# A hand-ordered four-layer kernel: last front stores issued by GpSimd, front loads asked for a period ahead, four page turns first, one norm sum on VectorE, new keys' shares on ScalarE

## The chip, the cores and the metric

One Trainium2 chip, one of its cores. The metric is device microseconds (us) of one execution, median of the runs shown. Everything is float32.

## The reference, cut to what matters

Four residual layers follow each other on x, 64 sequences of 32 tokens with 512 features:

```python
x = x + einsum('bct,bcd->bdt', x, W0[cond])            # a 32x32 mix of the tokens of each sequence
x = x + x @ base_w.T + base_b + (x @ A[adapt].T) @ Bw[adapt].T      # LoRA, rank 16
# attention with a paged cache: 32 query heads, 8 key heads, D = 128
q, k, v = x @ Wq.T, x @ Wk.T, x @ Wv.T
q = rope(rmsnorm(q, q_norm_w), pos); k = rope(rmsnorm(k, k_norm_w), pos)
k_all = concat(k_cache[block_table], k); v_all = concat(v_cache[block_table], v)   # 512 + 32 keys
p = softmax(where(valid, q @ k_all.T / sqrt(D), -1e30))
x = x + (p @ v_all) @ Wo.T
x = x + einsum('bct,bcd->bdt', x, W3[cond])
```

rmsnorm(t, w) is t * rsqrt(mean(t*t) + eps) * w; rope multiplies by a cosine, a half-swapped copy by a sine, and adds the two.

## The kernel before

**Tiles.** The 2048 tokens are 16 tiles (`t`) of 128 tokens, four sequences each. The key heads are taken in two groups `g` of four. A *unit* is one sequence with one group of key heads (128 units), and it takes four *slots*, one for each key head: 512 slots, 0 to 511, in which TensorE does scores, transposes of the probabilities and the product with the values. In the same slots the projections of the next pair of tiles are done (a pair has 32 slots): seven blocks of products with sums of weights (`block_sum`), their results taken from one PSUM bank (`proj_ps`) by `Block.take` on VectorE, then normed and rotated by class `Norm`.

**The front.** Slots -43 (`begin`) to -1 hold everything ahead of the first scores: layers 1 and 2 of all 16 tiles (class `First`), the turning of group 0's cached keys, 16 pieces of 128 rows (class `Turn`: load `page_rows`, four transposes into the one PSUM tile `s_ps`, copy back by ScalarE, store to DRAM as `kT`), the rotary tables (`rotary`, stored as `rot`), and the projections of the first pair. A tile of `First` starts every two slots; its slot `home` is -39 + 2t. Its steps are load, mix and add; `turn_x` (four transposes of x into the PSUM tile tagged "tx") and `keep_x` (ScalarE's copy to `x1T`); `ranks` (x1T times the LoRA factors, four products, also tagged "tx"); `linear` (chunks 0 to 4 into `l_ps`); the second `add`; `turn_out` and `keep_out` (PSUM tag "to"); `store_x`, `store`, and for odd tiles `sums` and `store_sums`. An even tile also turns its LoRA rows, `turn_a`/`keep_a`, through the same tag "to". Every PSUM tile named here has one buffer.

**What sets the order.** Nothing is scheduled by the compiler: each engine runs its instructions in the order in which they were emitted. `at(slot, where, do)` puts a call on a list, and `slot(i)` emits slot i in a fixed order of lists: fetch (SyncE's loads), pool (GpSimd), scores and flips of the attention, "pe", "power", one `norm_piece`, "turn", values, the division of the softmax, "dve", two more `norm_piece`, "keep", "act", "store". A call that waits holds up all that was emitted after it on the same engine; SyncE (SP) issues most transfers, GpSimd (POOL) the gathers and some weights. `norm_piece` takes the next of the queued VectorE pieces of the norms, at most two in a slot together with the takes counted in `busy`.

**Memory.** `x_sb` has 4 buffers, `page_rows` 4, `rot` 2, `rot_b` 2, `x_12` and `x_34` (the sums) 1. The pools of the front are closed at slots -7 (`start`) and -2 (`first`), and the attention's tiles `pen`, `sm`, `v_sb`, `v_new` lie in their memory: the first writer of these waits until the last reader of the old tiles is done. `Unit` issues 16 loads of `kT`, `Unit.mask` writes `pen` on GpSimd, which the first VectorE operation on the scores (`tensor_tensor_reduce`, L825) reads.

Of the kernel before, what the change touches and what calls it, by code (L numbers as in the profile page):

```python
# [43 lines left out]
P = 128  # L44
# [4 lines left out]
D = 128  # L49
# [28 lines left out]
def resid_kernel(  # L78
# [149 lines left out]
    with ExitStack() as l2:  # L228
# [161 lines left out]
        class First:  # L390
# [121 lines left out]

            def store_x(self):
                nc.sync.dma_start(out=x_dram[self.t], in_=self.x)

            def store(self):
                nc.sync.dma_start(out=xT_dram[self.t], in_=self.x2T)

            def store_sums(self):
                for i in (0, 1):  # L520
                    nc.sync.dma_start(out=xS_dram[self.t // 2][:, i], in_=self.s[i])
# [154 lines left out]
        class Norm:  # L676
# [35 lines left out]
            def swapped(self):  # L712
                which = 3 if self.k is None else 1
                self.b = proj_pool.tile([P, REP, D], F32, name="rot_b", bufs=2)
                half = D // 2
                for i in (0, 1):
                    nc.vector.tensor_tensor(
                        self.b[:, :, i * half : (i + 1) * half],
                        self.raw[:, :, (1 - i) * half : (2 - i) * half],
                        self.step.rot[:, which, i * half : (i + 1) * half]  # L720
                        .unsqueeze(1)
                        .to_broadcast([P, REP, half]),
                        ALU.mult,
                    )

            def sum(self):
                nc.gpsimd.tensor_tensor(self.a, self.a, self.b, ALU.add)  # L727
# [24 lines left out]
        class Unit:  # L752
# [85 lines left out]
            def divide(self, k):  # L838
# [4 lines left out]
                nc.vector.tensor_scalar(self.new[:, k, :], sm[:, L:], share, None, ALU.mult)  # L843
# [85 lines left out]
        def norm_piece(slot):  # L929


            if not pieces or pieces[0][0] > slot or busy.get(slot, 0) >= 2:
                return
# [3 lines left out]
            if norm:  # L937
                norm.sum()
                slot += 2
# [6 lines left out]
        def begin_norm(slot, norm):  # L946
# [3 lines left out]
            for piece in (norm.scale, norm.straight, norm.swapped):  # L950
                pieces.append((slot + 2, piece, norm if piece == norm.swapped else None))
# [30 lines left out]
        for i in range(n_pairs):  # L982
# [19 lines left out]
            if p == 0:  # L1002
# [3 lines left out]
                for w, what in zip((-1, 0, 2, 5) if g == 0 else (-12, -11, -10, -9), (3, 2, 1, 4)):  # L1006
                    at(home + w, "dve", block_sum, KV, what)
            if p == NT // 2 - 1:
# [14 lines left out]
        for t in range(NT):  # L1023
# [3 lines left out]
            at(home - 3 if t > 1 else begin, "fetch", call, *f, "load")  # L1027
            at(max(begin, home - 4), "pool", call, *f, "fetch")
# [11 lines left out]
            at(home + 2, "pe", call, *f, "linear", (0, 1, 2))  # L1040
            at(home + 3, "pe", call, *f, "linear", (3, 4))
            at(home + 3, "power", call, *f, "add")
            at(home + 4, "store", call, *f, "store_x")
            at(home + 4, "turn", call, *f, "turn_out")
            at(home + 4, "keep", call, *f, "keep_out")
            at(home + 5, "store", call, *f, "store")
            if t % 2:
                at(home + 5, "dve", call, *f, "sums")
                at(home + 6, "store", call, *f, "store_sums")
# [7 lines left out]
        for c in range(NT):  # L1057

            home = -27 + c
            key = -1 - c  # L1060
            at(home - 2 if c > 3 else begin + 8, "fetch", make, turn_of, key, Turn, 0, c, start_pool, 4)
            at(home, "turn", call, turn_of, key, "turn")
# [4 lines left out]
        for u in range(len(units)):  # L1067
            at(KG * (u - 1) if u > 1 else ready + 2 * u, "fetch", make, unit_of, u, Unit, u)
# [114 lines left out]
        with tc.manual_schedule(engines=ENGINES):  # L1183
# [20 lines left out]
            for j in (0, 1):  # L1204
                at(begin + 3, "store", load_kv_weights, 0, 1, j)
                at(begin + 4, "store", load_kv_weights, 0, 0, j)
# [243 lines left out]
```

## Time and profile before

| what | value |
|---|---|
| runs | 2533.17 us median of 3 (2532.82 to 2536.7) |
| profiled execution, its own time | 2537.45 us |
| its span, first to last instruction | 2535.6 us |
| TensorE busy | 2464.5 us (97%) |
| VectorE, ScalarE, GpSimd busy | 1717.2, 1305.9, 1303.7 us |
| slot 0's first scores start at | 204.83 us |
| last slots end, output projection begins | about 2150 us |

The span is told from the first instruction, and the execution's own time is 1.85 us longer. The profiled execution was 4.3 us slower than the median of the runs. "PE" is TensorE's products and transposes, "PEld" its weight loads, "SPq" SyncE's issue of transfers; "a <- b" says that a waited, and that b was what came last.

### The profile page before, as it was taken

To read this page: it belongs to the slowest core of one execution; us is meant where nothing else is said; L and a number is where in the kernel's file an instruction comes from. 1 tells how busy PE (TensorE), PEld (TensorE's weight loads), DVE (VectorE), ACT (ScalarE), POOL (GpSimd) and SP (SyncE) were. 2 spreads that over 40 slices of the span, in tenths; PEclk is the share of its full clock that TensorE was granted. 3 is DMA by queue.
4 is the path that set the end of the run, shared out by engine and by line. 5 is a ranking of instruction groups with operands and counts; after the bars stand their busy time and mean duration, and the time that the engine had idled before them with its cause. 6 is when DMAs were issued, how large, how long until landed. Compare 5 with 4: busy or idle time off the path is not lost.

```text
span 2535.6 us, 46991 instructions
## 1 busy us (share of the span) xinstructions
PE 2464.5 (97%) x13760; PEld 1861.5 (73%) x13760; DVE 1717.2 (68%) x4114; ACT 1305.9 (52%) x3623; POOL 1303.7 (51%) x1086
## 2 busy tenths in 40 slices
PE   7997999999999999999999999999999999999999
PEld 4554777777777776677777777777777778888887
DVE  6645877777777786888777777778777766433222
ACT  1234666666666665666666666666666654000000
POOL 4434666666656565666565666666566763000000
PEclk9998999999999999999999999999999999999999
DMA  6875666666666667766566656565657685333221
GB/s 228 271 224 159 184 199 191 196 185 197 185 191 188 195 190 225 216 200 184 176 188 183 186 168 190 170 186 170 189 170 219 214 277 155 126 108 127 100 84 59
DMA packets 442846, 459.68 MB, mean 181 GB/s; under 512 B 50720, under 2 KB 367008, under 8 KB 434784
## 3 DMA queue, kind: packets, MB, share of 16 engines
q1 hardware_dynamic: 393488, 294.38, 38.1%
q0 software_dynamic: 49104, 162.31, 21.1%
q8 instruction: 112, 1.84, 0.3%
q14 instruction: 142, 1.16, 0.2%
HBM read 385.18 MB, written 79.69 MB: 183 GB/s over the span
## 4 chain that ended last, share of the span: by engine, by line
PE 88%; DVE 5%; DMA 4%; SPq 1%; issue 1%; ACT 0%; POOL 0%; ACTq 0%; DVEq 0%; POOLq 0%
PE proj_ps L630 21%; PE o_ps L872 17%; PE out_ps L1274 14%; PE s_ps L817 10%; PE s_ps L820 8%; PE pT_ps L859 8%; PE head_ps L735 3%; PE o_ps L884 2%; PE l_ps L478 2%; DVE p_new L843 1%; DMA kT<-page_rows 1%; DVE sm L825 1%; DMA v_sb<-v,v_rows 1%; DMA x_sb<-in_x 1%; PE s_ps L852 1%
## 5 line engine op out<-in xcount | busy, mean ns | idle before, releaser
L872 PEld LDWEIGHTS o_ps<-pT,v_sb 128*128 128x128 f32 x4096 | 520.4, 192 | 135.2 <-issue 124.1
L105 POOL DMA_INDIRECT v_sb<-v,v_rows x512 | 525.6, 1027 | 182.1 <-PE o_ps L872 77.1
L825 DVE CUSTOM_DVE_ANT_0 sm<-s_ps,pen 128x544 f32<-128x544 f32 x512 | 369.4, 721 | 365.6 <-PE s_ps L820 250.4
L836 ACT ACTIVATE sm<-sm,top 128x544 f32<-128x544 f32 x512 | 382.2, 746 | 414.0 <-DVE top L825 305.9
L872 PE MATMUL o_ps<-pT,v_sb 128*128 128x128 f32 x4096 | 541.8, 275 | 5.9 <-DMA v_sb<-v,v_rows 5.5
L842 ACT ACTIVATE sm<-sm,share 128x512 f32<-128x512 f32 x512 | 369.9, 722 | 172.3 <-DVE share L841 139.5
L693 POOL TENSOR_TENSOR rstd<-ss,minus_half 128x4 f32<-128x4 f32 x160 | 198.5, 1241 | 368.0 <-DVE ss L691 365.5
L817 PE MATMUL s_ps<-kT,qT 128*128 128x288 f32 x1024 | 350.6, 424 | 13.7 <-DVE top L825 13.4
L861 DVE COPY pT<-pT_ps 128x512 f32<-128x512 f32 x512 | 350.6, 685 | 3.9 <-PE o_ps L872 1.5
L820 PE MATMUL s_ps<-kT,qT 128*128 128x256 f32 x1024 | 306.3, 381 | 2.5 <-DMA kT<-kT 2.5
L859 PE MATMUL pT_ps<-ident,sm 128*128 128x128 f32 x2048 | 308.2, 273 | 0.5 <-DVE pT L861 0.5
L727 POOL TENSOR_TENSOR rot_a<-rot_a,rot_b 128x512 f32<-128x512 f32 x160 | 205.6, 1285 | 197.2 <-DVE share L841 148.5
L859 PEld LDWEIGHTS pT_ps<-ident,sm 128*128 128x128 f32 x2048 | 256.4, 141 | 53.2 <-DVE pT L861 1.7
L788 POOL TENSOR_SCALAR pen<-key_f,seq_f 128x544 f32<-128x544 f32 x128 | 276.3, 2158 | 22.0 <-DMA xS<-x 11.0
L686 ACT ACTIVATE sq<-raw 128x128 f32<-128x128 f32 x640 | 198.1, 309 | 82.2 <-DVE raw L642 52.3
L820 PEld LDWEIGHTS s_ps<-kT,qT 128*128 128x128 f32 x1024 | 195.6, 191 | 57.3 <-issue 3.0
L642 DVE TENSOR_TENSOR raw<-proj_ps,raw 128x512 f32<-128x512 f32 x336 | 225.4, 682 | 8.4 <-PE proj_ps L630 6.0
L843 DVE TENSOR_SCALAR p_new<-sm,share 128x32 f32<-128x32 f32 x512 | 209.7, 410 | 18.1
L630 PE MATMUL proj_ps<-sum,x 128*128 128x512 f32 x384 | 192.1, 603 | 1.9 <-DVE raw L642 1.9
L105 POOL DMA_INDIRECT mix_rows<-in_w,cond_rows x32 | 33.7, 1055 | 309.0 <-DVE mix_diag L171 301.4
L817 PEld LDWEIGHTS s_ps<-kT,qT 128*128 128x128 f32 x1024 | 155.6, 192 | 33.2 <-DVE top L825 15.9
L1324 ACT COPY p<-out_ps 128x256 f32<-128x256 f32 x7 | 2.6, 372 | 333.1 <-PE out_ps L1274 333.1
(158 smaller groups left out, 3417.9 us busy)
## 6 DMA issues: line engine op xcount, KB each, us to landing
kT<-kT SPq DMA_DIRECT2D x2048, 64.0 KB
o<-oT SPq DMA_DIRECT2D x29, 1024.0 KB
o_in<-o SPq DMA_DIRECT2D x28, 1024.0 KB
rot<-rot SPq DMA_DIRECT2D x48, 256.0 KB
page_rows<-in_kv_cache SPq DMA_DIRECT2D x32, 256.0 KB
vn<-raw SPq DMA_DIRECT2D x32, 256.0 KB
v<-in_kv_cache SPq DMA_DIRECT2D x32, 256.0 KB
kT<-page_rows SPq DMA_DIRECT2D x32, 256.0 KB
```

The costliest lines, as they stand in the source:

```text
L105: nc.gpsimd.indirect_dma_start(out=dst, out_offset=None, in_=table, in_offset=bass.IndirectOffsetOnAxis(ap=index, axis=0),)
L630: nc.tensor.matmul(self.ps, lhsT=self.pair.x[x][:, c if x == "b" else half.start + c, :], rhs=blocks(self.b)[w][:, c, :], start=(c == 0), ...
L788: nc.gpsimd.tensor_scalar(self.pen, key_f, seq_f[:, self.b : self.b + 1], BIG, ALU.is_ge, ALU.mult)
L817: nc.tensor.matmul(ps[:, first:HID], lhsT=q, rhs=self.kT[:, :n1, k, :], start=True, stop=True)
L820: nc.tensor.matmul(ps[:, HID : first + LA], lhsT=q, rhs=self.kT[:, n1:, k, :], start=True, stop=True)
L825: nc.vector.tensor_tensor_reduce(out=sm, in0=ps[:, first : first + LA], in1=self.pen, scale=1.0, scalar=3e38, op0=ALU.add, op1=ALU.min, ac ...
L836: nc.scalar.activation(sm, sm, AF.Exp, bias=top, scale=-1.0, accum_out=total)
L842: nc.scalar.activation(sm[:, :L], sm[:, :L], AF.Copy, scale=share)
L859: nc.tensor.transpose(ps[:, c, :], self.sm[k][:, c * P : (c + 1) * P], ident)
L861: nc.vector.tensor_copy(pT, ps)
L872: nc.tensor.matmul(self.o_ps[k], lhsT=self.v[c][:, k * D : (k + 1) * D], rhs=self.pT[k][:, c, :], start=(c == 0), stop=False,)
L1274: nc.tensor.matmul(ps[:, :HALF], lhsT=o[:, i, :], rhs=w[i // REP][:, i % REP, :], start=(i == 0), stop=(i == KG * REP - 1),)
```

## The change

Eight edits. (1) The stores of the last three tiles of the front go through GpSimd's queue. (2) x of a tile is loaded at `home - 4` instead of `home - 3`, a page at its slot - 3 instead of - 2, with 5 buffers; `linear` and all that follows it is one slot earlier; tile 1's gathers are at `begin`. (3) Pages 0 to 3 are loaded at `begin` and turned in slots -40 to -37, at the head of the "pe" list from the second on, instead of in slots -27 to -24. (4) The key and value weights are loaded two slots later, and unit 1's `kT` one slot later. (5) The last sum of a norm is a fourth VectorE piece instead of a GpSimd operation, the heads are turned one slot after it instead of two, and `rot_b` has one buffer. (6) The new keys' shares are made by ScalarE. (7) Slots with a `block_sum` count as full for the norm pieces, every fourth slot may have one more piece, and (8) the key and value sums of group 1 stand in slots 204, 207, 210 and 213 instead of 211 to 214.

```diff
--- before.py
+++ after.py
@@ -510,15 +510,19 @@
                 if p == 0:
                     pair_of[0].x["12"], pair_of[0].x["34"] = s, r
 
+            def queue(self):
+
+                return nc.sync if self.t < NT - 3 else nc.gpsimd
+
             def store_x(self):
-                nc.sync.dma_start(out=x_dram[self.t], in_=self.x)
+                self.queue().dma_start(out=x_dram[self.t], in_=self.x)
 
             def store(self):
-                nc.sync.dma_start(out=xT_dram[self.t], in_=self.x2T)
+                self.queue().dma_start(out=xT_dram[self.t], in_=self.x2T)
 
             def store_sums(self):
                 for i in (0, 1):
-                    nc.sync.dma_start(out=xS_dram[self.t // 2][:, i], in_=self.s[i])
+                    self.queue().dma_start(out=xS_dram[self.t // 2][:, i], in_=self.s[i])
 
         lora = {}
         last_scores = []
@@ -711,7 +715,7 @@
 
             def swapped(self):
                 which = 3 if self.k is None else 1
-                self.b = proj_pool.tile([P, REP, D], F32, name="rot_b", bufs=2)
+                self.b = proj_pool.tile([P, REP, D], F32, name="rot_b")
                 half = D // 2
                 for i in (0, 1):
                     nc.vector.tensor_tensor(
@@ -724,7 +728,7 @@
                     )
 
             def sum(self):
-                nc.gpsimd.tensor_tensor(self.a, self.a, self.b, ALU.add)
+                nc.vector.tensor_tensor(self.a, self.a, self.b, ALU.add)
 
             def turn(self):
                 if "o" in room:
@@ -840,7 +844,7 @@
                 share = small.tile([P, 1], F32, name="share")
                 nc.vector.reciprocal(share, self.total[k])
                 nc.scalar.activation(sm[:, :L], sm[:, :L], AF.Copy, scale=share)
-                nc.vector.tensor_scalar(self.new[:, k, :], sm[:, L:], share, None, ALU.mult)
+                nc.scalar.activation(self.new[:, k, :], sm[:, L:], AF.Copy, scale=share)
 
             def flip_new(self):
 
@@ -929,14 +933,13 @@
         def norm_piece(slot):
 
 
-            if not pieces or pieces[0][0] > slot or busy.get(slot, 0) >= 2:
+            if not pieces or pieces[0][0] > slot or busy.get(slot, 0) >= 2 + (slot % 4 == 1):
                 return
             busy[slot] = busy.get(slot, 0) + 1
             _, piece, norm = pieces.pop(0)
             piece()
             if norm:
-                norm.sum()
-                slot += 2
+                slot += 1
                 while slot in turning or (slot - VLAG) % KG == KG - 1:
                     slot += 1
                 turning.add(slot)
@@ -947,8 +950,8 @@
 
             at(slot, "act", norm.squares)
             at(slot + 1, "power", norm.power)
-            for piece in (norm.scale, norm.straight, norm.swapped):
-                pieces.append((slot + 2, piece, norm if piece == norm.swapped else None))
+            for piece in (norm.scale, norm.straight, norm.swapped, norm.sum):
+                pieces.append((slot + 2, piece, norm if piece == norm.sum else None))
 
         def begin_block(pair, b, slots):
             block = Block(pair, b)
@@ -1003,8 +1006,10 @@
                 sums = [(b, what) for b in (0, 1) for what in (3, 2, 1)] + [(0, 4), (1, 4)]
                 for w, one in zip((5, 6, 7, 9, 10, 11, 17, 18), sums):
                     at(home + w, "dve", block_sum, *one)
-                for w, what in zip((-1, 0, 2, 5) if g == 0 else (-12, -11, -10, -9), (3, 2, 1, 4)):
+                    busy[home + w] = busy.get(home + w, 0) + 2
+                for w, what in zip((-1, 0, 2, 5) if g == 0 else (-19, -16, -13, -10), (3, 2, 1, 4)):
                     at(home + w, "dve", block_sum, KV, what)
+                    busy[home + w] = busy.get(home + w, 0) + 2
             if p == NT // 2 - 1:
 
                 if g == NG - 1:
@@ -1024,8 +1029,8 @@
             home = -WINDOW - AHEAD - 6 + 2 * t
             f = [first_of, t]
             at(home - 5 if t > 1 else begin, "fetch", make, *f, First, t)
-            at(home - 3 if t > 1 else begin, "fetch", call, *f, "load")
-            at(max(begin, home - 4), "pool", call, *f, "fetch")
+            at(home - 4 if t > 1 else begin, "fetch", call, *f, "load")
+            at(max(begin, home - 4) if t > 1 else begin, "pool", call, *f, "fetch")
             at(home - 2, "dve", call, *f, "diagonal")
             at(home - 1, "pe", call, *f, "mix")
             at(home - 1, "power", call, *f, "add")
@@ -1037,16 +1042,16 @@
             at(home + 1, "pool", call, *f, "bias")
             at(home + 1, "pe", call, *f, "ranks")
             at(home + 1, "power", call, *f, "own_ranks")
-            at(home + 2, "pe", call, *f, "linear", (0, 1, 2))
-            at(home + 3, "pe", call, *f, "linear", (3, 4))
-            at(home + 3, "power", call, *f, "add")
-            at(home + 4, "store", call, *f, "store_x")
-            at(home + 4, "turn", call, *f, "turn_out")
-            at(home + 4, "keep", call, *f, "keep_out")
-            at(home + 5, "store", call, *f, "store")
+            at(home + 1, "pe", call, *f, "linear", (0, 1, 2))
+            at(home + 2, "pe", call, *f, "linear", (3, 4))
+            at(home + 2, "power", call, *f, "add")
+            at(home + 3, "store", call, *f, "store_x")
+            at(home + 3, "turn", call, *f, "turn_out")
+            at(home + 3, "keep", call, *f, "keep_out")
+            at(home + 4, "store", call, *f, "store")
             if t % 2:
-                at(home + 5, "dve", call, *f, "sums")
-                at(home + 6, "store", call, *f, "store_sums")
+                at(home + 4, "dve", call, *f, "sums")
+                at(home + 5, "store", call, *f, "store_sums")
 
             home = SLOTS * t + 9
             turning.add(home)
@@ -1056,16 +1061,20 @@
             at(home + 1, "store", call, turn_of, t, "store")
         for c in range(NT):
 
-            home = -27 + c
+
+            home = -27 + c if c > 3 else begin + 3 + c
             key = -1 - c
-            at(home - 2 if c > 3 else begin + 8, "fetch", make, turn_of, key, Turn, 0, c, start_pool, 4)
-            at(home, "turn", call, turn_of, key, "turn")
+            at(home - 3 if c > 3 else begin, "fetch", make, turn_of, key, Turn, 0, c, start_pool, 5)
+            where = "turn" if c > 3 else "pe"
+            at(home, where, call, turn_of, key, "turn")
+            if 0 < c < 4:
+                plan[home, where].insert(0, plan[home, where].pop())
             at(home, "keep", call, turn_of, key, "keep")
             at(home + 1, "store", call, turn_of, key, "store")
             at(begin + 11 + c, "dve", rotary, c)
             at(begin + 11 + c, "store", store_rotary, c)
         for u in range(len(units)):
-            at(KG * (u - 1) if u > 1 else ready + 2 * u, "fetch", make, unit_of, u, Unit, u)
+            at(KG * (u - 1) if u > 1 else ready + 3 * u, "fetch", make, unit_of, u, Unit, u)
             at(KG * (u - 1) + 1 if u else -1, "pool", call, unit_of, u, "mask")
             for c in range(NC):
                 at(KG * u - 1 + c, "pool", call, unit_of, u, "fetch_values")
@@ -1202,8 +1211,8 @@
             nc.gpsimd.dma_start(out=lora["base"], in_=base_w)
             nc.gpsimd.dma_start(out=lora["bias"], in_=across(base_b, HID))
             for j in (0, 1):
-                at(begin + 3, "store", load_kv_weights, 0, 1, j)
-                at(begin + 4, "store", load_kv_weights, 0, 0, j)
+                at(begin + 5, "store", load_kv_weights, 0, 1, j)
+                at(begin + 6, "store", load_kv_weights, 0, 0, j)
             for c in range(2 * KG):
                 at(begin + 9 + c, "store", load_q_weights, 0, c // 2, c % 2)
             for i in range(begin + 1, begin + 11):
```

## Prediction

> **What bounds the kernel now.** First the page's busy shares and the row of slices, then the stages, then TensorE's waits in them.
>
> ```profile
> PE 2464.5 (97%) x13760; PEld 1861.5 (73%) x13760; DVE 1717.2 (68%) x4114; ACT 1305.9 (52%) x3623; POOL 1303.7 (51%) x1086
> PE   7997999999999999999999999999999999999999
> PEclk9998999999999999999999999999999999999999
> ...
> 104.00:170.00 66.00, 59.09 (x238) 33.58 (x237) 32.78 (x82) 20.61 (x60) 25.08 (x21) 0.95 0.78 245
> 180.00:200.00 20.00, 16.91 (x61) 8.49 (x59) 10.18 (x23) 6.74 (x23) 4.92 (x5) 0.98 0.36 113
> 200.00:220.00 20.00, 6.99 (x15) 3.35 (x14) 4.74 (x8) 3.67 (x11) 5.80 (x5) 0.67 0.48 149
> 300.00:400.00 100.00, 100.00 (x603) 75.18 (x602) 74.94 (x190) 64.45 (x175) 60.44 (x50) 1.00 0.65 189
> 1020.00:1040.00 20.00, 16.06 (x91) 11.20 (x89) 19.03 (x36) 10.34 (x30) 12.82 (x10) 1.00 0.78 246
> ```
>
> Columns of a stage: its length, busy time of PE, PEld, DVE, ACT, POOL, then the clock, the DMA share and GB/s. From 240 to 2150 us TensorE is the bound: in 300:400 it never idles, while VectorE has a quarter and ScalarE a third of the time free. So work moved between those engines is worth nothing there; time can come from the front (0 to 240) and from the few stages where TensorE idles, such as 1020:1040 (4 us, VectorE at 95%). In the front three things stand out.
>
> The largest hole is at the handover to the attention. In order of time (start, duration, engine, line, what it had waited for):
>
> ```profile
> 190.53 9.37 SPq L773 DMA_DIRECT2D kT<-kT  x16
> 201.80 9.34 SPq L773 DMA_DIRECT2D kT<-kT  x16
> 212.96 0.85 SPq L521 DMA_DIRECT2D xS<-x  x2
> 217.48 2.12 POOL L788 TENSOR_SCALAR pen<-key_f,seq_f 128x544 f32<-128x544 f32 x1 [10.99 <-DMA xS<-x]
> 220.41 1.33 PE L817 MATMUL s_ps<-kT,qT 128*128 128x288 f32 x2 [12.64 <-DVE top L825]
> ```
>
> SyncE issues 32 loads of kT, 0.59 us each, ahead of the last sums' store (212.96). `pen` lies in their memory, so GpSimd waits for that store to land, VectorE for `pen`, and TensorE 12.64 us for the one `s_ps`.
>
> The second is SyncE's queue between 104 and 170 us. Its waits (total, times, longest) and TensorE's there:
>
> ```profile
> SPq L256 <- DMA kT<-page_rows: 29.9, 11, 5.0
> SPq L399 <- DMA x<-x_sb: 25.0, 11, 5.6
> PE s_ps L272 <- DMA page_rows<-in_kv_cache: 3.6, 3, 2.4
> PE mix_ps L424 <- DMA x_sb<-in_x: 3.3, 3, 2.0
> ```
>
> A page's load stands behind the landing of the kT store that frees its buffer. From one page load to the one two later takes SyncE 13.6 us (107.87, 121.46, 135.01), TensorE wants 10.4 (turns of x2T at 73.09, 82.60, 93.97, 104.34). Over the five tiles from 104.34 to 169.35 the loss is 65.0 - 5 x 10.4 = 13 us. The third is the start: TensorE is busy 6.2 of the first 20 us.
>
> [...] clock 0.67 in 200:220, and four projection products take 3.78 us at 201.25 against 1.88. [...] p_new (L843) has median 242 and maximum 1358 ns, mean 410.
>
> **The change part by part.** Negative is faster.
>
> *Ring: stores through GpSimd, one slot earlier, unit 1 one slot later.* Ten DMAs leave SyncE; on GpSimd, at about 0.6 us of issue each (its base and bias issues), they are 6 us, in a stage in which it is busy 5 of 20. Behind them in its order stand `bias`, `power`, the gathers and `pen`, and each store waits for VectorE's `add` or `sums` or ScalarE's copy, all made a slot before it. The last sums go out in slot -4 instead of at 212.96, land some 4 us later (212.96 to 217), before `pen` comes up in slot -1. Removed: the wait of 12.6, and the half clock behind it (220.41 to 226: 0.7 + 0.5 + 0.9 + 0.7 + 0.3 = 3). What is late next is VectorE's chain of take, squares and norm, which already makes TensorE wait 2.31 + 0.79 at 197 to 201; I leave that. x2T of tile 15 moves one slot earlier, but the slots after it are thin and bound by that chain: 1.5 us more. Sum -17; bounds -8 (pen then waits for something else by half) and -20.
>
> *Pages and x a slot ahead, four pages first.* The kT waits fall from 11 to 7, since pages 5 to 8 take buffers freed early; SyncE still falls behind in those 7 slots by (13.6 - 10.4)/2 = 1.6, 11 us in all, but a load now has 3 slots (15.6 us) for a store and a load of 4.4 + 3.2 us: 8 us of slack instead of 3. Of the 13 lost some 10 come back; bounds -4 and -13. The turns of four pages, 0.44 us each on TensorE, move to slots -40 to -37, where TensorE waits anyway (3.4 us for a_rows before 13.15): -2.
>
> *Start.* The gather of tile 1's mix rows, issued at 9.34 behind the 1 MB of base weights and landed at 18.5, goes ahead of them, and 2 MB of weights go later. Against that, page 1's turn waits for ScalarE's copy of page 0 out of the one `s_ps`, page 2's for page 1's, with `ranks` and `linear` behind them in TensorE's order; and SyncE waits for each copy before it stores the page, with the weights, x of tile 3 and later stores behind. The weights then go out at about 20 us, the first sum of them is taken at 38.8. I take -2; bounds -6 and +4.
>
> *Two new waits of TensorE.* Before, chunks 3 and 4 of `linear` (1.72 us) stand between `turn_x` and `ranks` and cover ScalarE's copy. After, they come ahead of `turn_x`, and `ranks` follows it directly. And `turn_out` of an even tile now stands in the same slot as the next even tile's `turn_a`, both through "to", so `turn_a` waits for `keep_out`. The trace has the parts:
>
> ```profile
> 34.07 0.60 PE L441 MATMUL x1T_ps<-ident,x_sb 128*128 128x128 f32 x4
> 35.02 0.59 ACT L457 COPY x1T<-x1T_ps 128x512 f32<-128x512 f32 x1
> 35.37 1.02 PE L478 MATMUL l_ps<-b_rows,hT 128*128 128x512 f32 x2
> ```
>
> The next product could start 0.44 us after the turn starts (34.51); the copy lets it start after 0.60 + 0.09 + 0.59 + 0.07 = 1.35 us: 0.9 us lost. For `ranks` 15 tiles at 0.9, less 0.44 in some 10 slots where a page or a head is turned in between: 9 us. For `turn_a` 7 x 0.9 = 6. Behind them stands all of TensorE's order, and from 20 to 104 us it is busy 81.2 of 84, so nothing covers them; 1 us falls in waits that remain. Sum +14; bounds +5 (the copies are taken early) and +26 (ScalarE first does squares, 2 us a norm).
>
> *Norm's sum on VectorE, shares on ScalarE.* Off GpSimd go 160 sums of 1272 ns (L727); on VectorE each costs what its like costs (L705, 683 ns): +109 us. Off VectorE go 512 x 410 ns = 210 us. On ScalarE no 32-wide scaled copy is shown: [...] above, 282 + (722 - 570, what a scale costs on 512) = 434; I take 250, 128 us. All of it lies beside TensorE: VectorE gets 100 us lighter, ScalarE goes from 64 to about 71% in the main loop. A share is needed two slots later, by `flip_new`; a sum by the heads' turn a slot later. Zero by itself; bounds -4 (fewer of the 0.6 us waits for VectorE's takes) and +8 (if that cover is gone, takes stand behind sums).
>
> *Sums of weights spread, their slots kept free of norm pieces.* In 1020:1040 four sums of 1.22 us in four slots in a row fill VectorE, and TensorE loses 4 us, 6 with the later ones. The first now stands three slots behind the issue of its weights; the gather queued behind these landed by 991.8, about when slot 204 begins: no new wait. -5; bounds -7 and +3.
>
> **Sum.** -17 - 10 - 2 - 2 + 14 + 0 - 5 = -22, and 1 more from VectorE's relief in the front: -23. Against the profiled execution's own time, 2537.45, that is 2514.5; it was 4.3 above the median, so 2533.2 - 23 = **2510**.
>
> **Rivals.** *The new waits eat the front* (0.2): the two TensorE waits at their upper bound and the start at its: -17 - 10 - 2 + 4 + 26 - 5 = -4 to -10, 2523 to 2529. For it: one-buffer PSUM tiles. Against: ScalarE is busy 12 of 44 us there. *The ring's hole stays* (0.1): the stores do move, but `pen` stands behind them on GpSimd or on another old tile, and only 2 of the 17 come: 2525, with the upper waits (+12) 2537, no change. *VectorE comes late in the main loop* (0.15), the other side: a norm's four pieces come ahead of the take that frees `proj_ps`, and TensorE waits. Price: 160 sums of 0.68; with a third exposed 36 us, so 2546. It decides from 23/160 = 0.14 us a norm. Against: p_new's 0.41 a slot is gone, and the cap of pieces holds. *The forecast* has 0.55, 2497 to 2522.
>
> The range takes in the last two at their middle, 2494 to 2541. What a measurement can tell from no change is 0.2%, 5 us. Faster by more 0.75, within it 0.09, slower 0.16.
>
> **What would show it.** Right: `pen` waits under 2 us and slot 1's scores start at about 203; SyncE's wait for kT<-page_rows falls under 20 us and TensorE's for page_rows and x_sb to nearly nothing; new rows of TensorE waiting for x1T (L457) and for x2T's copy (L494), 14 us together; L597's slots with VectorE under 85%. Wrong: a hole before the first scores, or waits of proj_ps for L642 or the new sum above 20 us in 240 to 2100.

## The result and the profile after

| kernel | median of its runs, us | against before |
|---|---|---|
| before | 2534.93 (2532.82 to 2537.07, 4 runs) | 1 |
| after | 2504.18 (2501.93 to 2507.74, 4 runs) | 0.988 [0.9863, 0.9897] |

The change saves 30.75 us; 23 were forecast. The profiled execution's span went from 2535.6 to 2506.0 us, that is 29.6 less. The total came out near the forecast by luck, however: two errors in its sum cancel. Where slots and tiles start in the two traces shows the parts:

| from ... to | before, us | after, us | after less before |
|---|---|---|---|
| start ... x of tile 3 is turned | 42.7 | 50.3 | +7.6 |
| ... x of tile 15 is turned | 137.0 | 134.3 | -2.7 |
| ... scores of slot 16 | 97.9 | 86.3 | -11.6 |
| ... slot 192 | 663.3 | 656.0 | -7.3 |
| ... slot 224 | 131.0 | 120.5 | -10.5 |
| ... slot 256 | 122.9 | 127.5 | +4.6 |
| ... output projection | 956.5 | 947.2 | -9.3 |
| ... end | 384.2 | 383.8 | -0.4 |

The front, to slot 16, gives 6.7 us of the 29.6, where the prediction had some 18; the main loop gives 22.5, where it had 5. The profile's page of after, busy shares, slices and clock:

```profile
PE 2450.6 (98%) x13760; PEld 1860.3 (74%) x13760; DVE 1628.5 (65%) x3762; ACT 1399.2 (56%) x4135; POOL 1131.3 (45%) x936
...
PE   7998999999999999999999999999999989999999
...
PEclk9999999999999999999999999999999999999999
```

TensorE goes from 97 to 98%; the three other engines together are busy 168 us less (VectorE 89 and GpSimd 172 less, ScalarE 93 more). TensorE's own busy time falls by 13.9 us with the same 13760 instructions; this page doesn't tell why. The stages of after (length, then busy PE, PEld, DVE, ACT, POOL; clock; DMA share; GB/s):

```profile
20.00:60.00 40.00, 33.22 (x114) 17.33 (x114) 25.77 (x51) 8.84 (x13) 14.49 (x12) 0.96 0.64 210
104.00:170.00 66.00, 62.93 (x259) 36.01 (x257) 43.67 (x96) 21.13 (x60) 25.93 (x21) 1.00 0.82 264
...
200.00:220.00 20.00, 15.10 (x38) 7.45 (x38) 13.71 (x32) 9.81 (x30) 12.48 (x11) 0.74 0.59 175
300.00:400.00 100.00, 100.00 (x602) 75.62 (x601) 70.60 (x172) 70.72 (x211) 52.38 (x42) 1.00 0.64 189
1000.00:1020.00 20.00, 20.00 (x118) 14.76 (x117) 15.37 (x36) 14.30 (x44) 13.35 (x13) 1.00 0.84 266
```

In 20:60 TensorE is busy 33.2 us at a clock of 0.96, against 39.6 us at 1.00 before: that is the slower start. In 104:170 it is busy 62.9 against 59.1. At 1000:1020 stand the slots that stood in 1020:1040 before: no idle time is left, and VectorE is at 77%. At the handover to the attention, in order of time:

```profile
194.66 9.93 SPq L777 DMA_DIRECT2D kT<-kT  x16
...
201.90 1.08 POOL L525 DMA_DIRECT2D xS<-x  x2
...
203.85 3.75 PE L634 MATMUL proj_ps<-sum,x_b 128*128 128x512 f32 x4 [3.66 <-DVE raw L646]
...
205.81 9.32 SPq L777 DMA_DIRECT2D kT<-kT  x16
...
211.91 2.42 POOL L792 TENSOR_SCALAR pen<-key_f,seq_f 128x544 f32<-128x544 f32 x1
...
215.58 0.65 PE L821 MATMUL s_ps<-kT,qT 128*128 128x288 f32 x2
```

The store of the last sums now leaves through GpSimd at 201.90, between the two blocks of loads, and `pen` (211.91) has no wait behind it. Slot 1's scores start at 215.58, 4.8 us earlier than before and not at 203: the norm chain on VectorE is next, with a wait of 3.66 us, and the clock is low around it (0.50 in 203.85:207.70, 0.74 in 200:220): four products take 3.75 us. Two waits of SyncE in the front of after (total, times, longest):

```profile
SPq L399 <- DMA x<-x_sb: 15.4, 9, 3.0
SPq L256 <- DMA kT<-page_rows: 14.7, 7, 3.3
```

SyncE's longest wait there is now another: 21.4 us, in ten times, for the rotary tables that VectorE makes and SyncE stores (8.0 us in two before).

And TensorE's in the whole of after:

```profile
PE h_ps L462 <- ACT x1T L457: 8.2, 14, 1.4
PE mix_ps L424 <- DVE mix_diag L415: 7.8, 1, 7.8
PE proj_ps L634 <- DVE raw L646: 7.1, 7, 3.7
PE aT_ps L441 <- ACT x_a L494: 4.8, 7, 0.7
```

### The profile page after: what moved, and what is told of

Same layout as the page of the kernel before. It is cut to its first block, busy times and chain, and to the rows that moved or that the text cites. A ratio compares the mean times of both kernels' runs of the same rounds, so it can differ in the third digit from the quotient of the medians.

```text
span 2506.0 us, 47285 instructions
## 1 busy us (share of the span) xinstructions
PE 2450.6 (98%) x13760; PEld 1860.3 (74%) x13760; DVE 1628.5 (65%) x3762; ACT 1399.2 (56%) x4135; POOL 1131.3 (45%) x936
## 4 chain that ended last, share of the span: by engine, by line
PE 92%; DMA 2%; SPq 2%; issue 1%; DVE 1%; ACT 1%; POOL 0%; DVEq 0%; ACTq 0%
PE proj_ps L634 22%; PE o_ps L876 17%; PE out_ps L1283 15%; PE s_ps L821 10%; PE s_ps L824 8%; PE pT_ps L863 8%; PE head_ps L739 3%; PE l_ps L478 3%; PE o_ps L888 2%; SPq L777 1%; DMA kT<-kT 1%; PE h_ps L462 1%; PE proj_ps L1116 1%; PE s_ps L856 1%; PE mix_ps L1301 1%
## 5 line engine op out<-in xcount | busy, mean ns | idle before, releaser
L697 POOL TENSOR_TENSOR rstd<-ss,minus_half 128x4 f32<-128x4 f32 x160 | 208.2, 1301 | 525.8 <-DVE ss L695 525.7
L792 POOL TENSOR_SCALAR pen<-key_f,seq_f 128x544 f32<-128x544 f32 x128 | 286.3, 2237 | 10.8
L1283 PE MATMUL out_ps<-w,o_in 128*128 128x256 f32 x768 | 167.1, 379 | 0.0
L1283 PEld LDWEIGHTS out_ps<-w,o_in 128*128 128x128 f32 x768 | 145.9, 190 | 19.8
```

The costliest lines, as they stand in the source:

```text
L792: nc.gpsimd.tensor_scalar(self.pen, key_f, seq_f[:, self.b : self.b + 1], BIG, ALU.is_ge, ALU.mult)
L1283: nc.tensor.matmul(ps[:, :HALF], lhsT=o[:, i, :], rhs=w[i // REP][:, i % REP, :], start=(i == 0), stop=(i == KG * REP - 1),)
```

## Experiments

Every ratio is against the kernel before, run beside it, with its 95% interval. "A pair" is the time in which 32 slots pass, in the undisturbed part of group 0 and then of group 1: 120.56 and 120.04 us before, 119.20 and 118.33 after. Six pairs of each make (1.36 + 1.71) x 6 = 18 us of difference.

### The new keys' shares and the norm's last sum

**The shares back on VectorE, in after.**

```diff
-                nc.scalar.activation(self.new[:, k, :], sm[:, L:], AF.Copy, scale=share)
+                nc.vector.tensor_scalar(self.new[:, k, :], sm[:, L:], share, None, ALU.mult)
```

> The changed kernel with one thing put back: the new keys' shares (p_new) on VectorE again; the norm's sum stays on VectorE. Theory A (in the kernel before, a p_new that ran beside GpSimd's norm sum was stretched from 0.24 to 1.35 us and held up the take that frees proj_ps, so it takes both together to lose time): a pair's 32 slots stay at about 119.2 us in group 0 and 118.3 in group 1, p_new has a mean near 0.30 (only those beside GpSimd's pen are long), and the time is within 4 us of the changed kernel. Theory B (VectorE's load as such set the pace): VectorE is now heavier than in either kernel, a pair takes 120.5 or more, the time is 15 to 20 us above the changed kernel.

Measured: 0.9892 [0.9874, 0.9911]; a pair takes 119.65 and 118.47 us. p_new takes 289 ns in the mean, at most 723. So with the sum gone from GpSimd the shares on VectorE cost (0.45 + 0.14) x 6 = 3.5 us, although VectorE is busy 1744.7 us here, more than in before or after. Its load as such is not what costs the pairs of before their time.

**The sum back on GpSimd, in after,** at the same place in the order:

```diff
-                self.b = proj_pool.tile([P, REP, D], F32, name="rot_b")
+                self.b = proj_pool.tile([P, REP, D], F32, name="rot_b", bufs=2)
...
-                nc.vector.tensor_tensor(self.a, self.a, self.b, ALU.add)
+                nc.gpsimd.tensor_tensor(self.a, self.a, self.b, ALU.add)
```

> The changed kernel with one thing put back: the norm's sum on GpSimd again (emitted at the same place, rot_b with two buffers again); the shares stay on ScalarE. Theory A: no p_new stands on VectorE to be stretched, so a pair stays within 0.4 us of 119.2 and 118.3, and the time within 5 us of the changed kernel; VectorE's two-input operations may now and then be stretched. Theory B: VectorE is at its lightest, so the time is at or below that of the changed kernel. A theory that GpSimd's work alone costs TensorE time wants 120.0 or more for a pair.

Measured: 0.9914 [0.9893, 0.9936]; a pair takes 119.20 to 119.60 and 118.33 to 118.51 us, so in the steady part nearly nothing is lost. Of the 10 us by which its profiled execution is longer than after's, 4.3 lie in slots 192 to 224 (124.8 against 120.5 us, where TensorE once waits 2.3 for gathered values) and 4.1 behind slot 476; their cause stays open. As for VectorE's two-input operations, in the trace of before two of them beside this sum (L698 at 221.62 and L705 at 205.40) take 2.45 and 1.64 us, where their medians are 0.68.

**Both back, in after:** the two edits above together.

> The changed kernel with both put back: shares on VectorE and the norm's sum on GpSimd (rot_b with two buffers); order of the pieces, caps and all of the front as in the changed kernel. Theory A: the stretched p_new is back, mean about 0.41, a pair takes 120.3 to 120.6 in group 0 and about 120 in group 1, the time is 15 to 20 us above the changed kernel, although each of the two alone costs under 5. Rival C (the gain came from the new order of the pieces and heads, not from the engines): a pair stays at 119.2 and the time within 4 us.

Measured: 0.9936 [0.9912, 0.996], some 14 us above after, with intervals that are apart. So the time is near theory A's, but it is not lost where theory A put it: a pair takes 119.48 and 118.6 to 118.9 us, p_new 347 ns in the mean. That is only 0.3 of the 1.36 us that a pair of before takes longer. Of the 19 us by which the profiled execution is longer than after's, the steady pairs make some 4, slots 192 to 224 make 5.2, slots 224 to 256 2.4 and slot 0 2.0; most of the rest lies behind slot 476. Why these stages lose is open. In the steady pairs, with both instructions where they were, most of the gain stays: in after the pieces of the norms stand in other slots, and the sum is a piece of its own behind `rot_b`. That the order is a second way to this part of the gain is argued from this and not tested by itself; the engines alone don't explain it. Nor does the whole time show that it takes both: alone the two cost some 3 and 9 us, together 14.

**Before, with the shares on ScalarE and nothing else.** This is the first diff of this section the other way round, in the kernel before.

> The kernel before with one part of the change: the new keys' shares on ScalarE. Theory A' (in the order of the kernel before, GpSimd's sum starts with p_new, stretches it to 1.35 us, and the take behind it comes late): without p_new on VectorE the wait in slot 20 of a pair (4.84 us against 3.97) is gone, a pair takes 119.2 to 119.6 instead of 120.56, the time falls by 12 to 18 us. Theory C' (only the new place of the sum does it, some other VectorE operation is stretched in its place): a pair stays above 120.2 and the time within 6 us of before.

Measured: 0.9895 [0.9878, 0.9911], so this one line brings 1.05% of 2538, 27 us of after's 31. A pair takes 119.20 and 118.33 us, to the hundredth what after has: 18 us. Another 6 lie in slots 192 to 224 (124.97 against 131.03 us). The hole at the handover stays (`pen` waits 10.8 us). One slot shows how. In before, in order of time (start, duration, engine, line, what it had waited for):

```profile
412.60 0.65 PE L817 MATMUL s_ps<-kT,qT 128*128 128x288 f32 x2
...
412.72 1.35 DVE L843 TENSOR_SCALAR p_new<-sm,share 128x32 f32<-128x32 f32 x1
412.77 1.27 POOL L727 TENSOR_TENSOR rot_a<-rot_a,rot_b 128x512 f32<-128x512 f32 x1 [1.78 <-DVE share L841]
...
413.99 0.68 DVE L642 TENSOR_TENSOR raw<-proj_ps,raw 128x512 f32<-128x512 f32 x1
...
414.72 1.98 PE L630 MATMUL proj_ps<-wq,x_a 128*128 128x512 f32 x4 [0.61 <-DVE raw L642]
...
417.44 0.65 PE L817 MATMUL s_ps<-kT,qT 128*128 128x288 f32 x2
```

GpSimd's sum starts 0.05 us after p_new, and p_new takes 1.35 us instead of 0.24. The take (L642) stands behind it on VectorE, TensorE's next projection behind the take: the slot takes 417.44 - 412.60 = 4.84 us. The same slot with the shares on ScalarE:

```profile
413.49 0.65 PE L817 MATMUL s_ps<-kT,qT 128*128 128x288 f32 x2
413.50 0.67 DVE L642 TENSOR_TENSOR raw<-proj_ps,raw 128x512 f32<-128x512 f32 x1
...
413.67 1.27 POOL L727 TENSOR_TENSOR rot_a<-rot_a,rot_b 128x512 f32<-128x512 f32 x1 [1.78 <-DVE share L841]
...
414.85 1.88 PE L630 MATMUL proj_ps<-wq,x_a 128*128 128x512 f32 x4
...
417.46 0.65 PE L817 MATMUL s_ps<-kT,qT 128*128 128x288 f32 x2
```

GpSimd's sum is still there, 1.27 us as before. But the take starts at once, the projection waits for nothing, and the slot takes 3.97 us. These 0.87 us are in every pair; slots 1 and 2 of a pair give 0.33 and slot 8, whose take also follows p_new, 0.15.

**Before, with the sum on VectorE and nothing else.**

```diff
-                nc.gpsimd.tensor_tensor(self.a, self.a, self.b, ALU.add)
+                nc.vector.tensor_tensor(self.a, self.a, self.b, ALU.add)
```

> The kernel before with one part of the change: the norm's sum on VectorE, at the place where GpSimd's was issued, behind the swapped halves and ahead of the division. Theory A': the stretch is gone, p_new's mean falls to about 0.29, but a sum of 0.68 now stands where the stretch of 1.1 stood, so about half of the gain: a pair at 119.7 to 120.1, the time 5 to 12 us below before. Theory C': a pair stays above 120.4. My rival of the prediction (sums ahead of takes cost TensorE) wants more than 120.8 and a time above before.

Measured: 0.9936 [0.9919, 0.9952]; a pair takes 119.88 and 119.49 us, p_new 262 ns. So p_new is short again once GpSimd has no sum beside it. Of the 512 in before, 62 were held by that sum and took 1.22 to 1.36 us: in each of them the sum started between 0.08 us ahead of p_new and 0.05 us behind it, and p_new ended 0.04 us after the sum. In 40 others the sum started 0.06 us or more behind p_new, and p_new took its 0.24 us. Beside `pen` 61 took longer too, 0.72 us at most. The sum on VectorE gives about half the gain in the pairs, since a sum of 0.68 us now stands in the slots itself.

### The handover: stores and unit 1's loads

**All stores of the front on SyncE, in after.**

```diff
-                return nc.sync if self.t < NT - 3 else nc.gpsimd
+                return nc.sync
```

> The changed kernel with one thing put back: all stores of the front on SyncE's queue. Theory D (the 32 loads of kT ahead of the last sums' store made pen wait): the store goes out only behind unit 0's loads, some 5 us later than now, or behind both units' loads where one slot decides it; pen waits 4 to 12 us and the time is 4 to 12 us above the changed kernel. Rival E (the store's one slot earlier and unit 1's one slot later did it, the queue is irrelevant): pen waits under 1 us and the time is within 2 us.

Measured: 0.9885 [0.9862, 0.9908]; `pen` waits 0.1 us, slot 1's scores start at 215.23. The queue that the change is named for makes no difference by itself: with unit 1's loads a slot later, the store stands ahead of them on SyncE too (206.43).

**Unit 1's kT loads where they were, in after** (stores through GpSimd):

```diff
-            at(KG * (u - 1) if u > 1 else ready + 3 * u, "fetch", make, unit_of, u, Unit, u)
+            at(KG * (u - 1) if u > 1 else ready + 2 * u, "fetch", make, unit_of, u, Unit, u)
```

> The changed kernel with one thing put back: unit 1's kT loads in slot -4 instead of -3 (stores of the last tiles still through GpSimd). Theory D' (the hole needs both: unit 1's loads ahead of the last sums' store in one queue): no hole, pen waits under 1 us, time within 3 us of the changed kernel. Rival E' (the unit's slot alone decides it): pen waits 4 us or more and the time is 4 to 12 us above.

Measured: 0.9884 [0.9866, 0.9903]; `pen` waits 0.1 us, slot 1's scores start at 214.49.

**Both of these edits.**

> The changed kernel with two things put back: unit 1's kT loads in slot -4, and all stores of the front on SyncE's queue. Theory D': now the last sums' store stands behind both units' loads again, it goes out about 10 us later, pen waits 4 us or more, slot 1's scores start 4 to 10 us later than the changed kernel's 215.6, and the time is 4 to 12 us above it. Rival E'' (the tile's one slot earlier is enough): pen under 1 us and the time within 3 us.

Measured: 0.9919 [0.9903, 0.9936]. The hole is back, in order of time:

```profile
207.41 9.37 SPq L777 DMA_DIRECT2D kT<-kT  x16
...
217.66 0.81 SPq L525 DMA_DIRECT2D xS<-x  x2
...
221.96 2.12 POOL L792 TENSOR_SCALAR pen<-key_f,seq_f 128x544 f32<-128x544 f32 x1 [9.23 <-DMA x_b<-xT]
...
224.89 1.33 PE L821 MATMUL s_ps<-kT,qT 128*128 128x288 f32 x2 [8.23 <-DVE top L829]
```

The store stands behind the second block of loads, `pen` waits 9.23 us for the memory, and slot 1's scores start 9.3 us later than in after. So the GpSimd queue and the later loads do the same thing twice, and either is enough. Against after's own 0.988 [0.9863, 0.9897] the hole costs 0.0039, some 10 us; the two intervals just miss each other.

### The front: pages and order

**Pages 0 to 3 turned in their old slots, in after.**

```diff
-            home = -27 + c if c > 3 else begin + 3 + c
+            home = -27 + c
...
-            at(home - 3 if c > 3 else begin, "fetch", make, turn_of, key, Turn, 0, c, start_pool, 5)
-            where = "turn" if c > 3 else "pe"
+            at(home - 3 if c > 4 else begin + 8, "fetch", make, turn_of, key, Turn, 0, c, start_pool, 5)
+            where = "turn"
```

> The changed kernel with one thing put back: pages 0 to 3 turned in slots -27 to -24 again (the first five loaded in slot -35; five buffers and loads three slots ahead stay). Theory F (the early pages made the start slow: each page's turn waits for ScalarE's copy out of the one s_ps, and TensorE runs cold behind it): x1T of tile 3 comes at about 45 us instead of 50.3, SyncE's waits for kT<-page_rows rise from 7 to about 11 but TensorE's for page_rows stay under 2 us, the time is 2 to 6 us below the changed kernel. Rival G (the pages filled idle time; the slow start is that of the new order of linear and ranks): x1T of tile 3 within 1 us of 50.3, and the time 1 to 8 us above, since 1.8 us of turns and the queue's waits come back.

Measured: 0.9891 [0.9876, 0.9905], span 2505.9 us; x of tile 3 is turned at 50.0 us (50.3 in after), slot 16 starts at 269.9 (270.9). TensorE in the start of this kernel, in order of time:

```profile
26.98 1.16 PE L462 MATMUL h_ps<-x1T,aT 128*128 128x128 f32 x8 [0.68 <-ACT x1T L457]
31.00 4.32 PE L478 MATMUL l_ps<-base_sb,x1T 128*128 128x512 f32 x6 [2.86 <-DVE x_sb L433]
...
37.51 0.66 PE L441 MATMUL aT_ps<-ident,a_rows 128*128 128x128 f32 x4 [0.68 <-ACT x_a L494]
...
41.74 1.16 PE L462 MATMUL h_ps<-x1T,aT 128*128 128x128 f32 x8 [1.42 <-ACT x1T L457]
```

The late start is all there without a page turn in it, as rival G had it. So the page turns in front are neither its cause nor a gain that can be measured. What is there is the product for tile 1 (L478) at 31.00, after 2.86 us for VectorE's `add` of tile 0. It started at 30.96 in before as well, since that `add` ends only then; but before had the mix of tile 2 and the turn of LoRA rows ahead of it, and waited 0.44. Behind the longer wait the six products take 4.32 us instead of 2.84: the clock is 0.96 in 20:60, as in after (where it is 0.76 in 30:37), and 1.00 in before. One thing more is in this run: SyncE waits 11 times for kT again, 27.2 us in all, and x of tile 15 is turned at 185.6 us, only 1.1 later than in after.

**The front's old order too, in after:** the pages as above, x loaded at `home - 3`, and `linear` and all that follows it one slot later; the buffers and the pages' loads 3 slots ahead stay.

```diff
-            at(home - 4 if t > 1 else begin, "fetch", call, *f, "load")
+            at(home - 3 if t > 1 else begin, "fetch", call, *f, "load")
...
-            at(home + 1, "pe", call, *f, "linear", (0, 1, 2))
-            at(home + 2, "pe", call, *f, "linear", (3, 4))
+            at(home + 2, "pe", call, *f, "linear", (0, 1, 2))
+            at(home + 3, "pe", call, *f, "linear", (3, 4))
...
```

> The changed kernel with the front's old order: linear and what follows it one slot later, x loaded three slots ahead, pages 0 to 3 at their old slots. What is left of the change in the front: the page loads three slots ahead with five buffers, tile 1's gathers early, weights two slots later, the last stores through GpSimd, unit 1 a slot later. If the front's new order costs more than it brings: x1T of tile 15 by 172 us or earlier instead of 184.6, pen waits under 4 us, the time 5 to 14 us below the changed kernel. If the old order needs the loads a slot earlier: SyncE's waits are back, x1T of tile 15 later than 177 us, and the time within 4 us or above.

Measured: 0.9871 [0.9857, 0.9886], span 2506.4 us; that is after's time within the intervals. But it gets there by another way: x of tile 3 is turned at 40.9 us, of tile 8 at 92.0 (105.7 in after), and of tile 15 at 185.2 (184.6). Two stages of it:

```profile
20.00:60.00 40.00, 38.48 (x146) 21.28 (x145) 29.93 (x70) 8.93 (x14) 17.88 (x15) 1.00 0.70 236
...
104.00:170.00 66.00, 53.16 (x197) 29.91 (x196) 32.58 (x78) 17.06 (x53) 18.68 (x17) 0.90 0.76 235
```

In 20:60 TensorE is busy 38.5 us, 5.3 more than in after; in 104:170 it is 53.2, 9.8 less. Its waits:

```profile
PE mix_ps L424 <- DMA x_sb<-in_x: 10.9, 5, 4.9
...
PE h_ps L462 <- ACT x1T L457: 0.7, 1, 0.7
```

The wait for x1T is gone, and that for ScalarE's `x_a` does not occur at all; the time is lost to x of a tile that has not landed, and x is also loaded a slot later here. Against this order the new TensorE waits cost the total nothing that can be seen: a front that runs ahead of SyncE's loads is held by these. What they cost beside the earlier loads is not shown, since the old order with x loaded a slot earlier was not tried.

**Mix first in its slot, LoRA rows turned a slot later, in after,** meant to put other products into the two new waits:

```diff
+            plan[home - 1, "pe"].insert(0, plan[home - 1, "pe"].pop())
...
-                at(home - 1, "turn", call, *f, "turn_a")
-                at(home - 1, "keep", call, *f, "keep_a")
+                at(home, "turn", call, *f, "turn_a")
+                at(home, "keep", call, *f, "keep_a")
```

It changes the computation: at that slot the name of the LoRA rows already stands for those of the next pair of tiles, so these are turned, and the turn waits for a gather issued in the same slot.

> The changed kernel with TensorE's order mended at two places: mix of the next tile ahead of ranks, and turn_a one slot later, ahead of turn_x, so that neither follows directly the copy it waits for. Theory H (the two new waits lie fully on the path: 8.2 us for x1T and 4.8 for x2T's copy): both rows fall under 3 us, tile 15's x1T comes 8 to 11 us earlier than 184.6, the time is 7 to 11 us below the changed kernel. Rival I (what waits less there waits at the next step, for VectorE's add or its mix_diag): the rows fall but new rows of mix_ps or l_ps take their place, and the time is within 3 us.

Measured: 0.9943 [0.993, 0.9956]; slot 16 starts at 285.6 us. TensorE's waits:

```profile
PE mix_ps L424 <- DVE mix_diag L415: 18.2, 9, 2.6
PE aT_ps L441 <- DMA a_rows<-in_lora_a,lora_rows: 11.8, 2, 8.2
...
PE h_ps L462 <- ACT x1T L457: 0.6, 2, 0.4
```

The wait for x1T is covered (0.6 us), but the mix now comes before VectorE has made its `mix_diag` and waits 18.2 us. The 11.8 us for `a_rows` belong to the changed gather. The two can't be taken apart in one time, so this says only that mix can't stand there for nothing.

**The same with the pages in their old slots.**

> Both of the others together: mix ahead of ranks and turn_a a slot later, and pages 0 to 3 at their old slots. Theories F and H both right: the gains add up, 10 to 16 us below the changed kernel, about 2490. F wrong: no better than mix and turn_a alone.

Measured: 0.9941 [0.9929, 0.9954], with 24.4 and 17.2 us of the same two waits. It adds that the pages make no difference here either.

## Why the prediction was right and where it was wrong

**Right in the total, wrong in the main loop.** "Zero by itself", with a lower bound of -4, was the largest error: after gains 18 us in twelve steady pairs, and the edit on the shares alone has the same pairs. Two readings failed. The first is "in 300:400 it never idles". That stage of 100 us lies within one period of 120.56, and the slow slots start at 292.05 and 412.60, one on either side of it. The stage of a whole period of before shows it:

```profile
300.00:420.56 120.56, 119.95 (x719) 89.95 (x718) 91.80 (x232) 79.52 (x223) 74.51 (x61) 1.00 0.66 192
```

Idle for 0.61 us in each pair, the wait of slot 20. The second is that TensorE's busy time is taken at its word. The slot was 0.87 us longer than without that cause, and slots 1, 2 and 8 show no idle time and are yet 0.48 us longer together, under a busy row of 100% in 300:400: the busy row does not show what these slots lose. A row on the page of before had a sign of it. The chain that ended last, by engine:

```profile
PE 88%; DVE 5%; DMA 4%; SPq 1%; issue 1%; ACT 0%; POOL 0%; ACTq 0%; DVEq 0%; POOLq 0%
```

and by line it gave p_new (L843) 1.0%, 25 us, at a place where it took 1.35 us. With the shares on ScalarE, in the kernel before:

```profile
PE 91%; DMA 3%; DVE 2%; SPq 1%; issue 1%; POOL 1%; ACT 0%; ACTq 0%; POOLq 0%
```

VectorE falls from 5 to 2% of the chain, 3% of 2536 us being 76 us, and the kernel is 27 us faster: what goes from the chain is partly replaced by TensorE. I had the long p_new before me, 1358 ns against a median of 242, and costed its mean of 410 as work beside TensorE, without asking who stood behind it on VectorE. The trace shows that a p_new which starts with the sum lasts until the sum's end, 1.35 us instead of 0.24; by what means the sum holds it is not shown. The path through the take is what the runs add.

**The ring, -17, was mis-sized.** `pen` waits 0.1 us, as forecast, and from slot 0 to slot 16 the kernel takes 58.1 us instead of 72.8: 14.7 less, near the 12.6 + 3 of my sum (the clock is 0.50 in 220.41:226 of before, where I took the 3). But from x of tile 15 to slot 0 it takes 28.2 us instead of 25.1, 3.1 more where I had taken 1.5 off, so the whole comes to -11.6; the runs with and without the hole differ by 10. The term that failed is "I leave that", the chain of take, squares and norm. In before it stood like this:

```profile
197.92 2.54 PE L630 MATMUL proj_ps<-sum,x_b 128*128 128x512 f32 x4 [2.31 <-DVE raw L642]
```

In after the same wait is 3.66 us and the block behind it takes 3.75, 2.6 us more together; the next block takes 3.78 us in both. The clock is 0.50 in 200:206 of before, behind waits of 2.31 and 0.79 us, and 0.50 in 203.85:207.70 of after, behind one of 3.66. Also, what brings the gain is not GpSimd's queue as such: the same time comes from unit 1's later loads.

**The start, -2 with bounds -6 and +4, had the wrong cause and sign.** It is +7.6 to tile 3. I blamed the page turns in my upper bound; with the pages in their old slots it is still +7.3. In that run TensorE's waits up to the turn of tile 3 are 4.6 us longer than in before: 2.8 by the two new ones and 2.4 by the wait for tile 0's `add`, 0.6 less by others. The other 2.7 are busy time: four products of `linear`, some 1.7 us, which now stand ahead of that turn, and products at the lower clock (4.32 us instead of 2.84). So it is, as far as the waits tell, the earlier `linear`, which meets tile 0's `add` with nothing left ahead of it. That `add` comes late because VectorE works from 24.80 to 30.26 us without a pause on tables and row numbers that stand ahead of it. The run with the early start undid the order and x's earlier loads together, so the two are not told apart.

**The two new TensorE waits, +14, were right in size:** 8.2 us in 14 waits for x1T (0.7 in one before) and 4.8 in 7 for `x_a`, 13.0. Their net cost is another matter. With them gone and x loaded a slot later the front ends at the same time, because loads of x are late instead.

**SyncE's queue, -10, was right in kind; its size is open.** Seven waits for kT instead of 11, 14.7 us, as forecast; no wait of TensorE for the landing of `page_rows` or x remains, 6.9 us in before. From tile 3 to tile 15 the kernel gains 2.7 us in spite of some 10 us of new waits. That would leave 13 for the queue, but only if the new waits are a full loss. And the fall from 11 waits to 7 is not what counts: with the pages in their old slots they were 11 again, for 1.1 us. No run undid the earlier loads alone. Together all terms of the front but the ring stood at -1; x of tile 15 comes 4.9 us later.

**The weight sums, -5, came, but only in part from their new places.** In before slots 212 to 216 take 5.97, 4.16, 3.96, 6.80 and 3.59 us, in after 3.97, 3.22, 3.63, 4.51 and 3.11: 6.0 less. But in the kernel before with the shares on ScalarE and nothing else these slots are already 2.8 us shorter, so about 3.3 are left for the sums. The other 4.5 of the -10.5 between slots 192 and 224 are slot 200, with a kT load that lands earlier (8.44 to 3.97 us). In the two kernels made from before slot 200 is short as well (4.61 and 4.11 us), so this is not the sums' doing, and its cause is open.

**"No new wait" was wrong, though.** Slots 235 and 236 take 8.32 and 5.64 us in after, 4.51 and 3.25 before: +6.2. In the trace of after, in order of time:

```profile
1061.93 1.09 DVE L709 TENSOR_TENSOR rot_a<-raw,rot 128x512 f32<-128x512 f32 x1
...
1072.64 11.69 SPq L579 DMA_DIRECT2D rot<-rot  x2
...
1083.22 0.75 DVE L721 TENSOR_TENSOR rot_b<-raw,rot 128x256 f32<-128x256 f32 x2
...
1086.47 9.38 SPq L777 DMA_DIRECT2D kT<-kT  x16
...
1096.46 0.72 PE L821 MATMUL s_ps<-kT,qT 128*128 128x288 f32 x2 [4.09 <-DMA kT<-kT]
```

With slots counted as full for the norm pieces, the piece `rot_b` of a norm stands 21 us behind its `rot_a`; between them VectorE does four weight sums (L601, 1.22 us each) and takes. In before it came ahead of these sums. It is the last reader of the old `rot`, so SyncE's load of the new one (L579) holds the queue from 1072.64 to 1084.33, the loads of kT behind it go out late, and TensorE waits 4.09 us for one. In before the same load went out at once:

```profile
1097.55 0.91 SPq L575 DMA_DIRECT2D rot<-rot  x2
```

The ten kernels made from after, and after itself, take 7.8 to 8.7 us in slot 235; before and the two made from it 4.5 to 5.2. I left edit 7 with a bound of +3 and did not look for what the delayed piece frees. No run undid edit 7 alone, so that it is the cause is read from the wait and not tested. If it is, the term as a whole, put at -5, came out at zero or above. Slot 484 is also longer (+5.0), behind 17.7 us of issue for one block of kT loads; it varies from 3.2 to 9.8 between kernels made from after, and stays open.

**Page turns, -2:** nothing measurable. **The rivals:** of "the new waits eat the front" the mechanism came, at half its size, and the front still gained; the ring's hole did not stay. VectorE late in the main loop, the other side, did not come: the waits of proj_ps for the take fell from 19.6 us in 24 to 7.1 in 7.

## What to carry to other kernels

Before a stage is called bound by one engine, look at a whole period of it, and at the chain that ended last: a small row there of another engine, with a maximum far above its median, can be a stall that the busy row hides, as p_new was here (1.0% of the chain, median 242 and maximum 1358 ns, under a busy row of 100%). Ask of a slow instruction what stands behind it on its engine, not only what share of the time it takes. And two edits that both remove one hole are worth that hole once; only the run with neither shows it.

## What the runs showed of the hardware that was not expected

In before, the copy of 32 elements a partition with a scale (p_new) takes 242 ns on VectorE in the median, and up to 1358 ns when GpSimd's sum of 512 elements starts with it. It is not overlap as such that costs: all 62 copies that the sum preceded, or followed within 0.05 us, lasted to the sum's end, and all 40 that had started 0.06 us or more ahead of the sum took 0.24 to 0.25 us. On ScalarE the same copy takes 304 to 311 ns in all 512 cases of after, and in all 512 of the kernel before with that one line changed, where 147 ran beside the sum; the 250 I had taken was an estimate, since before has no such copy: its copies of 128 elements without a scale take 251 to 282 ns (means of L854, L898, L804). The sum costs 1272 ns on GpSimd and 0.69 us on VectorE (medians).
